# A graph layer's gather of x[src]: more columns copied by ScalarE and VectorE, with 16-bit addresses

## The chip, the cores and the metric

The kernel runs on one core of one Trainium2 chip. A core has TensorE (matmuls, with their weight loads), VectorE (DVE in the profile), ScalarE (ACT), GpSimd (POOL) and SyncE (SP), each with its own instruction stream, and 16 DMA engines that move data when one of these streams issues a transfer. The time is device microseconds of one execution; the figure given is the median of several runs.

## The reference

There are 12,500 nodes with 64 features and 400,000 edges, sorted by their target `dst`. An edge's message is a two-layer network of the features of its source, of its target and of 16 edge attributes; messages are summed per target, and each node is updated and normalised.

```python
m_in = jnp.concatenate([x[src], x[dst], edge_attr], axis=-1)
h = jax.nn.silu(m_in @ W1 + b1)
messages = jax.nn.silu(h @ W2 + b2)
agg = jax.ops.segment_sum(messages, dst, num_segments=x.shape[0])
node_in = jnp.concatenate([x, agg], axis=-1)
return jax.nn.silu(node_in @ W3 + b3)
...
x = _layernorm(x + _L0_gnn_ref(x, edge_index, edge_attr_16, ...), axis=-1)
```

All is float32.

## The kernel before, in words

**Tiles and octets.** The 3,125 tiles of 128 edges are worked in 391 octets of 8 tiles (1,024 edges); three octets are a chunk. Because the edges are sorted by target, an octet touches a window of at most 48 consecutive nodes. A loop over `o` (line 626) issues the work of all stages, each stage for another octet; its engines TensorE, ScalarE, VectorE and SyncE run exactly the order that is written there (`manual_schedule`), and each of these streams is in order. The pools' buffer counts (lines 251 to 261) decide how far one stage may run ahead of the next.

**The part of x[src].** Before the loop has got far, the product of all x with the first 64 rows of W1 is put into a table `pa` in DRAM (`table`, lines 178 to 192). From octet 12 on (`RAW`), a tile's 128 rows of that table come in one of three ways:

- POOL issues one indirect DMA for a tile (`gather`, line 396), three octets ahead (`AHEAD`), into a tile `ga` of five buffers. TensorE transposes them into the PSUM tile `p1` (line 476).
- For one pair of tiles (256 edges) of some octets, listed in `pairs`, the features are copied column by column out of `xs`, which holds x transposed (a feature per partition, a node per column of 4 bytes). Each copy moves one node's column, 64 partitions by 4 bytes, to its edge's place in the tile `cx`: on VectorE a `tensor_reduce` (line 301), on ScalarE a `copy` (line 303). The address of the column is in a register. Registers are filled by a load of up to 16 addresses at a time (line 294; `LOADS` says how many by the first load of a part and by its later ones), which the engine's sequencer carries out itself. TensorE then multiplies `cx` by W1 (line 479).
- For one pair of tiles of some other octets, listed in `rpairs`, SyncE copies single rows of `pa`, 16 in each octet (`rows`, line 347).

**Addresses.** `index` loads the 256 source numbers of a pair as int32 into a tile `cxi` of one partition (SyncE, three octets ahead). `address` (line 382, VectorE, two octets ahead) turns them in place into byte addresses: 4 times the number plus `XADDR`, where `xs` begins in a partition. `xs` is held twice, in partitions 0 to 63 and 64 to 127; the first 128 edges of a pair are copied from the lower copy and the last 128 from the upper, whose address carries the partition in its upper bits (`XBASE`). `resident` (line 146) loads both copies.

**How columns are dealt out.** `ACOLS` and `VCOLS` give the columns per octet: ScalarE 32 ahead of its silu `h` (line 483) and 28 ahead of its silu `m` (line 498); VectorE 32 between `oh` and `xw`, and 32 behind `eh`. The sum, `RATE`, is 124. A pair takes part in the octet that comes one octet after its last column could be written.

**The other stages of an octet.** SyncE loads the targets of a chunk into `dr` and its attributes into `oh` (`load`, lines 435 and 436, two octets before the chunk; two buffers each) and the window's x into `xr` (line 415, three octets ahead). VectorE adds the sums of an octet six back to `agg` (line 512), compares targets with window nodes (`oh`, line 447, one octet ahead; `eh`, line 453), and masks the window's product (`xw`, line 425). TensorE, by octet: the window's product (line 420), transposes or column products of the sources, window and attributes (line 480), the sums of the octet four back (line 507), the bias and second layer of the octet two back (lines 492 and 494). ScalarE: columns, `h`, columns, `m`.

**Nodes.** 25 groups of up to 512 nodes are finished as soon as their sums are complete, one about every 16 octets: load, product on TensorE (`node_product`, lines 541 and 542, into a PSUM tile of the pool `mis` with two buffers, which the window products use too), silu on ScalarE (`node_silu`, line 548), statistics, division and store. `todo` lists them by octet; they come at the end of that octet's work, silu directly behind the product.

Of the kernel before, what the change touches and what calls it, by code (L numbers as in the profile page):

```python
# [9 lines left out]
F32 = mybir.dt.float32  # L10
BF16 = mybir.dt.bfloat16
I32 = mybir.dt.int32
U8 = mybir.dt.uint8
AF = mybir.ActivationFunctionType
OP = mybir.AluOpType
AX = mybir.AxisListType
# [2 lines left out]
ENG = mybir.EngineType  # L19

P = 128
# [9 lines left out]
LAST = 6  # L31
RAW = 12
TABLES = 7
ACOLS = (32, 28)
VCOLS = (32, 32)
ROWS = 16
LOADS = (16, 8)
XBASE = (0, 64 << 18)
XADDR = 36864
LAG = CT * P // 32  # L40

U = 125
# [58 lines left out]
def windows(ctx, tc, ident, badi, pa, x, xt, src_c, src_row, dst_c, dst_row, attr_t, dst_2, attr_2, base, w1, b1, w2, b2, w3, b3, out, edges):  # L101
    nc = tc.nc
    N, D = x.shape
    NP = xt.shape[1]
    A = attr_t.shape[0]
    TILES = edges // P
    NO = base.shape[1]
    assert 2 * (S + A) == P and N + S <= NP
    E = 2 * S
    const = ctx.enter_context(tc.tile_pool(name="fconst", bufs=1))  # L110

    fast = ctx.enter_context(tc.tile_pool(name="fast", bufs=1))
    scp = ctx.enter_context(tc.tile_pool(name="scp", bufs=3))
    srcs = {}

    def sources(k, part=None):
# [22 lines left out]
    for s in range(2):  # L139
        h = slice(s * D, (s + 1) * D)  # L140
        nc.scalar.dma_start(w1d[h, h], w1[0:D, :])
        nc.scalar.dma_start(b1s[h, :], b1.rearrange("(k o) -> k o", o=1))
    XC = 2048
    xs = fast.tile([P, NP], F32, name="xs")

    def resident(s, c):
        w = min(XC, NP - c)
        nc.scalar.dma_start(xs[s * D:(s + 1) * D, c:c + w], xt[:, c:c + w])

    resident(0, 0)  # L150
    for s in range(2):
        h = slice(s * D, (s + 1) * D)
        nc.scalar.dma_start(w2d[h, h], w2)
    resident(0, XC)
    w3x = const.tile([D, D], F32, name="w3x")
    b3r = const.tile([1, G, D], F32, name="b3r")

# [88 lines left out]
    octs = []  # L246
# [4 lines left out]
    with tc.tile_pool(name="gat", bufs=AHEAD + 2) as gat, tc.tile_pool(name="drp", bufs=2) as drp, \  # L251
# [4 lines left out]
            tc.tile_pool(name="ps1", bufs=2, space=PSUM) as ps1, \  # L256
            tc.tile_pool(name="ps2", bufs=2, space=PSUM) as ps2, \
            tc.tile_pool(name="psa", bufs=1, space=PSUM) as psa, \
            tc.tile_pool(name="cx", bufs=4) as cx, tc.tile_pool(name="cxi", bufs=3) as cxi, \
            tc.tile_pool(name="rx", bufs=2) as rx, tc.tile_pool(name="rxi", bufs=2) as rxi, \  # L260
            tc.tile_pool(name="nx", bufs=2) as nx, tc.tile_pool(name="nv", bufs=1) as nv:
        got, loaded, made = {}, {}, {}
# [2 lines left out]
        RATE = sum(ACOLS) + sum(VCOLS)  # L265
        pairs = []
        while True:
            o = RAW + -(-2 * P * (len(pairs) + 1) // RATE) + 1
            if o >= len(octs) - 1:
                break  # L270
            pairs.append(o)
        cols, indices = {}, {}
        xb = xs.bitcast(U8)

        def columns(o, eng, part):
            if o < RAW:
                return
            lo = (o - RAW) * RATE
            if eng == ENG.Activation:
                lo, n = lo + sum(ACOLS[:part]), ACOLS[part]  # L280
            else:
                lo, n = lo + sum(ACOLS) + sum(VCOLS[:part]), VCOLS[part]
            hi, todo = lo + n, n
            while lo < hi:
                j, e0 = lo // (2 * P), lo % (2 * P)
                if j >= len(pairs):
                    return
                n = min(hi - lo, P - e0 % P, LOADS[lo > hi - todo])
                if pairs[j] not in cols:
                    cols[pairs[j]] = cx.tile([P, P], F32, name="cx")  # L290
                t = cols[pairs[j]].bitcast(U8)
                s = e0 // P
                h = slice(s * D, (s + 1) * D)
                _, regs = nc.values_load_multi_w_load_instructions(  # L294
                    indices[j][0:1, e0:e0 + n], engines=(eng,), min_val=XBASE[s] + XADDR,
                    max_val=XBASE[s] + XADDR + 4 * (N - 1), skip_runtime_bounds_check_because="src names a node")
                for e, r in zip(range(e0 % P, e0 % P + n), regs):
                    to, frm = t[h, 4 * e:4 * e + 4], xb[h, ds(r - (XBASE[s] + XADDR), 4)]
                    if eng == ENG.DVE:

                        nc.vector.tensor_reduce(to, frm[:, :, None], AX.X, OP.max)  # L301
                    else:
                        nc.scalar.copy(to, frm)  # L303
                lo += n


        def begun(o):

            first, behind = -(-(o - RAW) * RATE // (2 * P)), -(-(o + 1 - RAW) * RATE // (2 * P))
            return range(max(0, first), max(0, min(behind, len(pairs))))  # L310

        def index(o):
            for j in begun(o):
                t = cxi.tile([1, 2 * P], I32, name="cxi")
                e = octs[pairs[j]][1] * P
                nc.sync.dma_start(t, src_row[:, e:e + 2 * P])
                indices[j] = t

        def address(o):
            for j in begun(o):  # L320
                t = indices[j]
                for s in range(2):
                    h = slice(s * P, (s + 1) * P)
                    nc.vector.tensor_scalar(t[:, h], t[:, h], 4.0, float(XBASE[s] + XADDR), op0=OP.mult, op1=OP.add)

        rpairs = []
        while True:
# [48 lines left out]

        def address(o):
            for j in begun(o):
                t = indices[j]
                for s in range(2):  # L380
                    h = slice(s * P, (s + 1) * P)
                    nc.vector.tensor_scalar(t[:, h], t[:, h], 4.0, float(XBASE[s] + XADDR), op0=OP.mult, op1=OP.add)

        winrow, winreg = {}, {}
        sums = psa.tile([P, 4, S], F32, name="pg")
# [38 lines left out]
        def window_copy(o):  # L424
            nc.vector.tensor_tensor(xw[o % 3][:E, :], winrow.pop(o)[:E, :], mask[:E, :], op=OP.mult)  # L425

        def load(c, o0=0, o1=CT // OT):

            if c not in loaded:
                loaded[c] = (drp.tile([E, CT // 2 * P], I32, name="dr"), hot.tile([P, CT // 2 * P], F32, name="oh"))  # L430
            dr, oh = loaded[c]
            e = slice(o0 * OT // 2 * P, o1 * OT // 2 * P)
            d = slice(c * CT // 2 * P + e.start, c * CT // 2 * P + e.stop)
            for k in range(2):
                nc.sync.dma_start(dr[k * S:(k + 1) * S, e], dst_2[k:k + 1, d].to_broadcast([S, e.stop - e.start]))
            nc.sync.dma_start(oh[E:, e], attr_2[:, d])

# [12 lines left out]
        def compare_nodes(o):  # L450
            c, t0, n, first, last = octs[o]
            eh = ehp.tile([P, OT, S], F32, name="eh")
            nc.vector.tensor_tensor(eh[:, :n], row[:, None, :].to_broadcast([P, n, S]),  # L453
                                    rel[:, t0:t0 + n, None].to_broadcast([P, n, S]), op=OP.is_equal)
            hots[o].append(eh)
# [54 lines left out]
        def add_window(o):  # L510
            a = agg[:, ds(winreg.pop((ENG.DVE, o)), S)]
            nc.vector.tensor_tensor(a, a, sums[:, o % 4, :], op=OP.add)  # L512
# [32 lines left out]
        def node_silu(q):  # L545
            p = groups[q][1] // G
            z = nx.tile([P, G, D], F32, name="z")
            nc.scalar.activation(z[:p], nodes[q][1][:p], AF.Silu)
            nodes[q].append(z)
# [32 lines left out]
        due = [-(-(c + n + LAG) // STEP) for c, n in groups]  # L582
        NCH = octs[-1][0] + 1
        lead = {c: o for o, (c, t, n, first, last) in enumerate(octs) if first}
        todo = {}

        def later(o, f, *a):
            todo.setdefault(min(o, NO), []).append((f, a))
# [4 lines left out]
        for q in range(early):  # L593
            o = lead[due[q]] + LAST - 1 if q < rest else NO
            later(o - 1, node_load, q)
            later(o, node_product, q)
            later(o, node_silu, q)
            later(o + 2, node_stats, q)
        for q0, q1 in batches:
            o = lead[due[q1 - 1]] + LAST - 1  # L600
# [22 lines left out]
        with tc.manual_schedule(engines={ENG.PE, ENG.Activation, ENG.DVE, ENG.SP}):  # L623
            compare_dst(0)
            compare_nodes(0)
            for o in range(NO + THIRD):
# [5 lines left out]
                    nc.scalar.activation(agg[:, k:k + n], zero.to_broadcast([P, n]), AF.Copy)  # L632
                if o < 2:
                    for c in parts[2:5] if o == 0 else parts[5:]:
                        resident(0, c)
                if o == 3:
                    for s in range(2):
                        nc.scalar.dma_start(w3s[s * D:(s + 1) * D, :], w3[D:2 * D, :])
# [4 lines left out]
                if o == RAW:  # L643
                    nc.vector.memset(mv, 1.0)
                    nc.vector.memset(eps, 1e-5)
                if 5 <= o < 5 + (len(parts) + 1) // 2:
                    for c in parts[(o - 5) * 2:(o - 4) * 2]:
                        resident(1, c)
                index(o + 3)
                rload(o + 3)  # L650
                if o % (SCT // OT) == 6 and (o // (SCT // OT) + 1) * SCT < TILES:
                    sources(o // (SCT // OT) + 1)
                if o + AHEAD < NO:
                    gather(o + AHEAD)
                if o + 2 < NO and octs[o + 2][3] and o + 2:
                    load(octs[o + 2][0])
                if o + 3 < NO:
                    window_load(o + 3)
                if o + 1 < NO:
# [7 lines left out]
                columns(o, ENG.DVE, 0)  # L667
                if o < NO:
                    first_layer(o)
                if o == 0:  # L670
                    nc.vector.tensor_copy(b2r, b2p[:, None, :].to_broadcast([3, OT, D]))
                if o + 1 < NO:
                    window_copy(o + 1)
                    compare_nodes(o + 1)
                columns(o, ENG.DVE, 1)
                if o == 1:
                    relative(CT, SCT)
                if 10 <= o < 9 + len(cuts):
# [38 lines left out]

        for o in range(NO + THIRD - LAST, NO):
            add_window(o)
        for f, a in todo.get(NO, []):  # L720
            f(*a)
        for q in range(early, NG):
            node_load(q)
            node_product(q)
            node_silu(q)
            node_stats(q)
# [262 lines left out]
```

## Time and profile before

| | |
|---|---|
| median of 3 runs | 3,443.22 us (3,439.3 to 3,445.99) |
| profiled execution | 3,453.06 us, span of the profile 3,450.7 us |
| TensorE busy (weight loads) | 74% (48%), mean granted clock 0.68 |
| VectorE busy | 73% |
| ScalarE busy | 79% |
| POOL busy | 74% |
| 16 DMA engines | 67 GB/s on average |
| gathers of POOL | 2,619 from `pa`, 96 from x in the first 12 octets |
| columns | 24,032 on VectorE, 22,560 on ScalarE |

A group of the profile is read as: line, engine, operation, output and input, count, then busy time in us and mean ns of one, then the engine's idle time just before these instructions and what ended most of it. "issue" is idle time that ended without anything the profile shows as a wait. Register loads and the issue of DMAs do not count as busy; the view of a single line shows them, with their durations. Copies of columns overlap in their engine: one takes 188 ns from start to end on ScalarE, while the next starts about 93 ns after it.

### The profile page before, as it was taken

To read this page: it belongs to the slowest core of one execution; us is meant where nothing else is said; L and a number is where in the kernel's file an instruction comes from. 1 tells how busy PE (TensorE), PEld (TensorE's weight loads), DVE (VectorE), ACT (ScalarE), POOL (GpSimd) and SP (SyncE) were. 2 spreads that over 40 slices of the span, in tenths; PEclk is the share of its full clock that TensorE was granted. 3 is DMA by queue.
4 is the path that set the end of the run, shared out by engine and by line. 5 is a ranking of instruction groups with operands and counts; after the bars stand their busy time and mean duration, and the time that the engine had idled before them with its cause. 6 is when DMAs were issued, how large, how long until landed. Compare 5 with 4: busy or idle time off the path is not lost. (4 is left out here: it accounts for less than half of the span.)

```text
span 3450.7 us, 104586 instructions
## 1 busy us (share of the span) xinstructions
PE 2554.8 (74%) x13750; PEld 1649.2 (48%) x13750; DVE 2517.4 (73%) x26396; ACT 2717.7 (79%) x23405; POOL 2569.0 (74%) x2724
## 2 busy tenths in 40 slices
PE   6877777777777677776777777777777677677777
PEld 4444544444445445444444445444445454444454
DVE  2477777777777777777777777777777777777775
ACT  2388788788887887888878888887788777878886
POOL 7777777777777777777777777777777777777773
PEclk9666667666667666776666666666666666766767
DMA  7423323323332332333332332333323323333322
GB/s 159 95 53 68 63 59 65 65 61 60 77 61 61 68 62 60 65 65 65 64 69 59 62 68 61 62 75 61 62 60 69 60 61 66 69 62 62 67 61 52
DMA packets 203931, 229.79 MB, mean 67 GB/s; under 512 B 133612, under 2 KB 141988, under 8 KB 202324
## 3 DMA queue, kind: packets, MB, share of 16 engines
q1 hardware_dynamic: 101528, 122.61, 16.1%
q0 software_dynamic: 86880, 89.14, 14.1%
q10 hardware_dynamic: 14812, 11.26, 1.4%
q14 instruction: 595, 4.87, 0.5%
q8 instruction: 116, 1.90, 0.2%
HBM read 216.36 MB, written 6.40 MB: 65 GB/s over the span
## 5 line engine op out<-in xcount | busy, mean ns | idle before, releaser
L396 POOL DMA_INDIRECT ga<-pa,sc x2619 | 2475.4, 945 | 802.2 <-issue 711.9
L303 ACT COPY cx<-xs 64x4 uint8 x22560 | 2216.5, 188 | 166.8 <-issue 122.0
L301 DVE TENSOR_REDUCE cx<-xs 64x4 uint8 x24032 | 1782.6, 150 | 544.7 <-issue 477.8
L507 PEld LDWEIGHTS pg<-eh,m 128*64 128x64 f32 x6250 | 301.0, 182 | 1046.8 <-issue 331.1
L507 PE MATMUL pg<-eh,m 128*64 128x48 f32 x6250 | 351.3, 271 | 580.9 <-DVE agg L512 523.0
L480 PE MATMUL p<-oh,xw 128*128 128x512 f32 (+1 forms) x758 | 601.0, 887 | 132.3 <-DVE xw L425 130.0
L494 PE MATMUL p<-w2d,h 128*128 128x128 f32 x3126 | 674.8, 383 | 0.0
L494 PEld LDWEIGHTS p<-w2d,h 128*128 128x128 f32 x3126 | 573.8, 275 | 133.1 <-issue 133.1
L498 ACT ACTIVATE m<-p 128x512 f32<-128x512 f32 x391 | 232.2, 594 | 255.5 <-PE p L494 249.0
L447 DVE TENSOR_TENSOR oh<-dr,wrow 96x512 f32<-96x512 int32 x391 | 264.4, 676 | 209.1 <-DMA dr<-in_dst 121.6
L483 ACT ACTIVATE h<-p,b1s 128x512 f32<-128x512 f32 x391 | 267.3, 684 | 139.2 <-PE p L480 86.1
L476 PE MATMUL p<-ident,ga 128*128 128x128 f32 x1310 | 336.9, 389 | 41.4 <-DMA ga<-pa,sc 41.4
L420 PE MATMUL mm<-w1bb,xr 64*96 64x128 f32 x782 | 252.9, 418 | 62.0 <-DMA xr<-in_xt 36.7
L476 PEld LDWEIGHTS p<-ident,ga 128*128 128x128 f32 x1310 | 199.6, 190 | 133.3 <-issue 110.3
L480 PEld LDWEIGHTS p<-oh,xw 128*128 128x128 f32 x758 | 176.7, 287 | 169.3 <-DVE xw L425 168.8
L453 DVE TENSOR_TENSOR eh<-wrow,dc 128x384 f32<-128x384 f32 x391 | 211.7, 541 | 0.0
L420 PEld LDWEIGHTS mm<-w1bb,xr 64*96 64x96 f32 x782 | 134.2, 224 | 140.2 <-issue 61.4
L492 PE MATMUL p<-b2r,one 3*128 3x512 bf16 x391 | 196.4, 502 | 0.0
L512 DVE TENSOR_TENSOR agg<-agg,pg 128x48 f32 x391 | 78.1, 200 | 74.2 <-PE pg L507 40.0
L479 PE MATMUL p<-cx,w1d 128*128 128x128 f32 x364 | 105.2, 387 | 22.7 <-ACT cx L303 22.7
L425 DVE TENSOR_TENSOR xw<-mm,mask 96x128 f32<-96x128 f32 x391 | 109.4, 280 | 13.4 <-PE mm L420 7.6
L396 POOL DMA_INDIRECT ga<-in_x,sc x96 | 91.5, 953 | 30.2 <-issue 27.7
(83 smaller groups left out, 767.6 us busy)
## 6 DMA issues: line engine op xcount, KB each, us to landing
rx<-pa SPq DMA_DIRECT2D x5888, 0.2 KB
dr<-in_dst SPq DMA_DIRECT2D x260, 288.0 KB
ga<-pa,sc POOLq DMA_INDIRECT x2619
oh<-in_attr SPq DMA_DIRECT2D x130, 192.0 KB
xr<-in_xt SPq DMA_DIRECT2D x391, 24.0 KB
xs<-in_xt ACTq DMA_DIRECT2D x12, 512.0 KB
pa<-v ACTq DMA_DIRECT2D x12, 256.0 KB
xa<-in_x SPq DMA_DIRECT2D x24, 128.0 KB
```

What stands on the lines that cost most here:

```text
L301: nc.vector.tensor_reduce(to, frm[:, :, None], AX.X, OP.max)
L303: nc.scalar.copy(to, frm)
L396: nc.gpsimd.indirect_dma_start(out=ga[:, i, :], out_offset=None, in_=x if o < RAW else pa[:, :], in_offset=bass.IndirectOffsetOnAxis(ap=sc ...
L420: nc.tensor.matmul(pw[:E, :], winrow[o].rearrange("k s w -> k (s w)"), w1bb.rearrange("k s m -> k (s m)"), start=True, stop=True)
L447: nc.vector.tensor_tensor(oh[:E, :], dr[:, e:e + w], wn[:E, o:o + 1].to_broadcast([E, w]), op=OP.is_equal)
L453: nc.vector.tensor_tensor(eh[:, :n], row[:, None, :].to_broadcast([P, n, S]), rel[:, t0:t0 + n, None].to_broadcast([P, n, S]), op=OP.is_equal)
L476: nc.tensor.matmul(p1[:, i, :], g2.rearrange("p s d -> p (s d)"), ident, is_transpose=True, start=(i == c), stop=False, skip_group_check=True)
L480: nc.tensor.matmul(p1[:, :k], xw[o % 3], oh, start=False, stop=True, skip_group_check=True)
L483: nc.scalar.activation(h[:, :k], p1[:, :k], AF.Silu, bias=b1s)
L494: nc.tensor.matmul(p2[:, 2 * i:2 * i + 2, :].rearrange("p s d -> p (s d)"), h[:, i, :], w2d, start=False, stop=(i == k - 1), skip_group_ch ...
L498: nc.scalar.activation(m[:, :n2], p2[:, :n2], AF.Silu)
L507: nc.tensor.matmul(pg[s * D:(s + 1) * D, :], m[:, i, :], eh[:, i, :], start=(i < 2), stop=(i >= n - 2), skip_group_check=True)
```

## The change

- **Addresses are 16-bit numbers.** `address` writes them to a new tile `cxa` (uint16, three buffers) in one instruction for all 256. To fit into 16 bits, `xs` moves to the front of SBUF (`XADDR` 8864 instead of 36864; its own pool is opened first, and the area for the descriptors of POOL's DMAs is cut to 8,192 bytes of a partition), and it is held once, in partitions 0 to 63. Columns of the last 128 edges of a pair are read there and written to partitions 64 to 127.
- **Loads.** Every load of addresses takes up to 16.
- **Columns.** ScalarE 72 (40 and 32), VectorE 88: 24 ahead of `xw`, 16 between `xw` and `eh`, 24 and 24 behind. `RATE` is 160.
- **An octet moved.** A pair takes part two octets after its last column could be written; `dr` and `oh` are loaded three octets before their chunk; `node_silu` stands behind the `h` of the next octet.
- **Buffers.** `cx` five instead of four, `cxi` two instead of three, `sc` two instead of three.

In ScalarE's order, an octet has two loads of 16 and one of 8 for the first 40 columns and two of 16 for the other 32; in VectorE's, each 24 columns have a load of 16 and one of 8. In the whole kernel, VectorE has 32,912 columns with 2,618 loads (1,496 of them ahead of 16 columns, 1,122 ahead of 8) where it had 24,032 with 2,391; ScalarE 26,992 with 1,968 where it had 22,560 with 2,352. POOL has 2,515 gathers from `pa`.

```diff
-ACOLS = (32, 28)
-VCOLS = (32, 32)
+ACOLS = (40, 32)
+VCOLS = (24, 16, 24, 24)
 ROWS = 16
-LOADS = (16, 8)
-XBASE = (0, 64 << 18)
-XADDR = 36864
+LOADS = (16, 16)
+XADDR = 8864
...
+    front = ctx.enter_context(tc.tile_pool(name="front", bufs=1))
+    xs = front.tile([P, NP], F32, name="xs")
...
-    scp = ctx.enter_context(tc.tile_pool(name="scp", bufs=3))
+    scp = ctx.enter_context(tc.tile_pool(name="scp", bufs=2))
...
-    def resident(s, c):
+    def resident(c):
         w = min(XC, NP - c)
-        nc.scalar.dma_start(xs[s * D:(s + 1) * D, c:c + w], xt[:, c:c + w])
+        nc.scalar.dma_start(xs[:D, c:c + w], xt[:, c:c + w])
...
-            tc.tile_pool(name="cx", bufs=4) as cx, tc.tile_pool(name="cxi", bufs=3) as cxi, \
+            tc.tile_pool(name="cx", bufs=5) as cx, tc.tile_pool(name="cxi", bufs=2) as cxi, tc.tile_pool(name="cxa", bufs=3) as cxa, \
...
-            o = RAW + -(-2 * P * (len(pairs) + 1) // RATE) + 1
+            o = RAW + -(-2 * P * (len(pairs) + 1) // RATE) + 2
...
                 _, regs = nc.values_load_multi_w_load_instructions(
-                    indices[j][0:1, e0:e0 + n], engines=(eng,), min_val=XBASE[s] + XADDR,
-                    max_val=XBASE[s] + XADDR + 4 * (N - 1), skip_runtime_bounds_check_because="src names a node")
+                    addresses[j][0:1, e0:e0 + n], engines=(eng,), min_val=XADDR,
+                    max_val=XADDR + 4 * (N - 1), skip_runtime_bounds_check_because="src names a node")
                 for e, r in zip(range(e0 % P, e0 % P + n), regs):
-                    to, frm = t[h, 4 * e:4 * e + 4], xb[h, ds(r - (XBASE[s] + XADDR), 4)]
+                    to, frm = t[h, 4 * e:4 * e + 4], xb[:D, ds(r - XADDR, 4)]
...
         def address(o):
             for j in begun(o):
-                t = indices[j]
-                for s in range(2):
-                    h = slice(s * P, (s + 1) * P)
-                    nc.vector.tensor_scalar(t[:, h], t[:, h], 4.0, float(XBASE[s] + XADDR), op0=OP.mult, op1=OP.add)
+                addresses[j] = cxa.tile([1, 2 * P], U16, name="cxa")
+                nc.vector.tensor_scalar(addresses[j], indices.pop(j), 4.0, float(XADDR), op0=OP.mult, op1=OP.add)
...
-            later(o, node_silu, q)
+            behind.setdefault(o + 1, []).append(q)
             later(o + 2, node_stats, q)
...
-                if 5 <= o < 5 + (len(parts) + 1) // 2:
-                    for c in parts[(o - 5) * 2:(o - 4) * 2]:
-                        resident(1, c)
...
-                if o + 2 < NO and octs[o + 2][3] and o + 2:
-                    load(octs[o + 2][0])
+                if o + 3 < NO and octs[o + 3][3]:
+                    load(octs[o + 3][0])
...
                 columns(o, ENG.DVE, 0)
                 if o < NO:
                     first_layer(o)
+                for q in behind.get(o, []) if o < NO else []:
+                    node_silu(q)
...
                 if o + 1 < NO:
                     window_copy(o + 1)
+                    columns(o, ENG.DVE, 1)
                     compare_nodes(o + 1)
-                columns(o, ENG.DVE, 1)
+                    columns(o, ENG.DVE, 2)
+                columns(o, ENG.DVE, 3)
...
+        for q in behind.get(NO, []):
+            node_silu(q)
         for f, a in todo.get(NO, []):
             f(*a)
+            if f is node_product:
+                node_silu(*a)
...
-    nc = bacc.Bacc("TRN2", target_bir_lowering=False, num_devices=1)
+    nc = bacc.Bacc("TRN2", target_bir_lowering=False, num_devices=1, dynamic_dma_scratch_size=8192)
```

## The prediction

> **What bounds the kernel now.** I read the page's busy shares first (they decide nothing: 73 to 79% on four engines), then the groups, the waits by engine, a table of nine 200 us stretches, and last the timeline of some octets.
>
> From the page, busy times and groups:
>
> ```profile
> PE 2554.8 (74%) x13750; PEld 1649.2 (48%) x13750; DVE 2517.4 (73%) x26396; ACT 2717.7 (79%) x23405; POOL 2569.0 (74%) x2724
> ...
> L396 POOL DMA_INDIRECT ga<-pa,sc x2619 | 2475.4, 945 | 802.2 <-issue 711.9
> L303 ACT COPY cx<-xs 64x4 uint8 x22560 | 2216.5, 188 | 166.8 <-issue 122.0
> L301 DVE TENSOR_REDUCE cx<-xs 64x4 uint8 x24032 | 1782.6, 150 | 544.7 <-issue 477.8
> ```
>
> The stretches (busy us and instruction counts of each engine), and the timelines of POOL and VectorE:
>
> ```profile
> 1000.00:1200.00 200.00, 143.41 (x776) 90.52 (x776) 148.97 (x1597) 162.15 (x1421) 151.19 (x161) 0.68 0.29 61
> 1800.00:2000.00 200.00, 146.13 (x791) 94.05 (x789) 149.19 (x1598) 166.68 (x1457) 151.21 (x161) 0.69 0.32 64
> ```
>
> ```profile
> 1603.21 0.94 POOL L396 DMA_INDIRECT ga<-pa,sc  x1 [0.30 <-issue]
> 1604.45 0.94 POOL L396 DMA_INDIRECT ga<-pa,sc  x1 [0.30 <-issue]
> ```
>
> ```profile
> 1614.11 1.00 DVE L572 TENSOR_SCALAR v<-v,mv,rstd 128x64 f32<-128x64 f32 x4
> 1615.03 0.19 DVE L512 TENSOR_TENSOR agg<-agg,pg 128x48 f32 x1
> 1615.15 0.67 DVE L447 TENSOR_TENSOR oh<-dr,wrow 96x512 f32<-96x512 int32 x1
> 1615.74 1.72 DVE L301 TENSOR_REDUCE cx<-xs 64x4 uint8 x24
> 1617.80 0.59 DVE L301 TENSOR_REDUCE cx<-xs 64x4 uint8 x8 [0.34 <-issue]
> 1618.32 0.27 DVE L425 TENSOR_TENSOR xw<-mm,mask 96x128 f32<-96x128 f32 x1
> 1618.51 0.54 DVE L453 TENSOR_TENSOR eh<-wrow,dc 128x384 f32<-128x384 f32 x1
> ```
>
> The reader should see that POOL issues 161 gathers in every 200 us, one each 1.242 us (0.94 busy, 0.30 between), whatever the rest does; waits of another kind are 62 us in the whole run. An octet has 8 tiles; 124 columns and 16 rows of it come another way, so POOL issues 8 - 140/128 = 6.906 gathers, which is 8.58 us an octet. 2,715 gathers are 3,372 of the 3,450.7 us. POOL bounds the kernel. The others follow by octet (23.3 octets in 200 us): ScalarE 163/23.3 = 7.0 us busy, VectorE 150/23.3 = 6.45 busy plus 477.8/379 = 1.26 "issue", TensorE 6.4. SyncE's 16 rows take 5.14, their address load 1.42, xr 0.65, with shares of dr, oh and cxi about 7.9.
>
> The "issue" idle is the address loads at L294, which the page does not count as busy. The view of that line, in narrow stretches of the trace (VectorE with 16 and with 8 addresses), the load of four window bases, and the lone load of one number at the end:
>
> ```profile
> L294 DVEq TENSOR_LOAD <-cxi x1: 1100/1100/1100, 1614.5 to 1614.5; - x1
> ...
> L294 DVEq TENSOR_LOAD <-cxi x1: 594/594/594, 1616.2 to 1616.2; - x1
> ...
> L404 DVEq TENSOR_LOAD <-bi x98: 340/344/761, 50.5 to 3424.8; - x98
> ...
> L95 DVEq TENSOR_LOAD <-badi x1: 309/309/309, 3442.9 to 3442.9; - x1
> ```
>
> **The change, part by part.**
>
> *More columns.* 160 instead of 124 per octet: 59,904 columns in place of 46,592, so 52 more pairs of tiles and 104 gathers fewer: 104 x 1.242 = 129 us off POOL, 8.23 us an octet. This is the ceiling of the gain.
>
> *ScalarE.* 12 more copies. In an uninterrupted row, 32 copies last 3.08 us, (3.08 - 0.19)/31 = 0.093 each: +1.12, 8.1 us busy. Of its idle time, the 122 us of "issue" shrink with shorter loads, and 123.2 us (24 waits of 5 us by z at L548 for the node product) go, because node silu now stands behind the next octet's h. What is late next there is m, which waits for TensorE today too (249 us). The product's PSUM buffer is held until then; the next TensorE instruction that takes it is the window product two octets on, so I cost the hold at nothing; without that cover it is the 26 us that L420 waits for z now. ScalarE comes to about 8.15.
>
> *VectorE.* 24 more reduces. Eight last 0.59 to 0.62 us with a 0.15 us tail, 0.064 each: +1.53 on 6.45 is 7.98. The addresses of a pair cost one instruction of 256 (333 ns by the like one at L363) instead of two of 128 (240 ns): 234 x 0.333 against 364 x 0.24, nothing. Decisive is what the loads now cost. Their number goes from 2,391 to 2,618 on VectorE (1,496 of 16 and 1,122 of 8) and from 2,352 to 1,968 on ScalarE. No row shows a 16-bit load. Its ends: 16 addresses cost between 594 ns (they are as many bytes as eight today) and 1,100; eight between 344 and 594. The rows for one, four, eight and sixteen numbers, 309, 344, 594, 1,100, are steps of about 250 per started four, and a single number costs nearly a full step. That looks like a read of 16 bytes at a time, with (344 - 309)/3 = 12 ns for each register. By bytes, 16 need two steps and eight more registers than the 594 row, some 690 at most. I take 650 and 370, nearer the low end.
>
> A load delays VectorE by what queued work does not cover. Today 1.26 us over 6.3 loads an octet. In the new order, 24 | xw | 16 | eh | 24 | 24 columns, loads behind oh (0.67) and eh (0.54, after 16 reduces) are covered; those behind xw (0.27) and behind eight reduces (0.51) stick out by 0.3 and 0.1. Four gaps fewer also take four tails of 148 - 64 = 84 ns out of the busy time. 7.98 + 0.4 - 0.34 = 8.05; with nothing exposed 7.6, with today's 0.2 per load 9.0.
>
> The sequencer alone: two loads of eight start 0.92 us apart, so eight reduces take it 0.04 us each. 1,496 x 0.65 + 1,122 x 0.37 = 1,387 us, 3.66 an octet, and 97 instructions 3.9: 7.55, less than 8.05.
>
> The Trainium skill, page "Runtime: NRT & Kernel Launch", section "Instruction fetch mechanics", prices such loads at about 200 ns per register, even in bulk. By that the width of a number would not matter; the rate itself is not that of the trace, 64 to 86 ns for four and more. The case is rival 3.
>
> *x once, at partitions 0 to 63.* Seven loads of x go, all in the first octets beside other work: 0, at most the 9.5 us that h once waited for a load of that queue. Half of the columns now read partitions 0 to 63 and write 64 to 127. No row shows that: at one end 0; at the other each such reduce waits for the one before, 148 instead of 64 ns, 44 x 0.084 = 3.7 us an octet. I take 0, as either half today runs at the 64 ns pitch.
>
> The Trainium skill, page "VectorE: DVE Perf Modes", section "Two Vector instructions with no wait between them", lets an instruction wait for its predecessors only if the quadrant of its input or of its output differs from the last one's. Inside a run of columns both stay the same, so by it the price is 0; no run here shows it yet.
>
> *dst an octet earlier.* The waits of oh for dr (121.6 us, 71 times) are largely gone where VectorE becomes late. With two buffers, the attr load must now wait until TensorE's L480 of the octet just before; behind it in SyncE's queue are xr and 16 rows. Held up to 3 us once in three octets, covered because xr is used two octets later and the rows a pair (16 octets) later; uncovered it is 1 us an octet. SyncE also issues 52 more cxi (0.25 each, 13 us, hidden), and loses its 44.7 us of waits for ScalarE to release cxi.
>
> *Pairs an octet later, five cx, two cxi, three cxa, two sc, a smaller descriptor area for POOL.* They move buffers, not work: 0. If POOL had to wait for descriptors, its 0.30 us gap would grow; 2,611 x 0.07 us would undo the gain. TensorE does 52 x 2 passes for 52 transposes more: 20 us beside its 26% idle.
>
> **Sum.** POOL 8.23, ScalarE 8.15, VectorE 8.05, SyncE 7.9: four in-order engines that lay 0.7 us and more below POOL come within 0.3 of each other. Octets are uneven (a node group adds about 5 us to TensorE once in 16), so I add 2%, an estimate: 8.40. (8.58 - 8.40) x 379 = 68 us. The profiled run took 3,453.06 us (2.4 around its span), so 3,385; the median of the runs is 10 lower: 3,375.
>
> **Rivals.**
> 1. POOL stays the only bound: 3,443 - 129 = 3,314. For: today it loses hardly anything to the others. Against: their margin falls from 8% to some 2%. 11%.
> 2. The engines hinder each other by 4% and more: 8.50 to 8.65, 3,413 to 3,470. For: the chain of waits already runs through dr, rows and TensorE, and L507 waits 523 us for agg on VectorE, which comes behind 48 more columns' worth of queue. 18%, and half of it is slower than before.
> 3. Slower: the load costs by the number of addresses. 1,496 x 1.1 + 1,122 x 0.597 = 2,315 us, 6.1 an octet, with 3.9 for the instructions 10.0 on VectorE's sequencer: +1.43 x 379 = 542, about 3,985. It decides from where loads exceed 8.58 - 3.9 = 4.7 us an octet, that is 16 addresses at some 830 ns. For: four addresses, not 16 bytes, explain the steps as well. Against: the near-equal price of one and four. 15%.
> 4. Reading and writing across partitions holds VectorE: 8.05 + 3.7 = 11.8, about 4,650. 4%.
>
> **How the numbers follow.** The forecast has 52%. The range 3,305 to 3,490 holds it and rivals 1 and 2; left out are 3 and 4, 19%. Within 0.2% (7 us, about what a measurement can tell here) only rival 2 falls: 5%. Faster: 52 + 11 + 5 = 68%. Slower: 8 + 15 + 4 = 27%.
>
> **What would show it.** Right: 2,611 gathers, still with mostly a 0.30 us gap but some waits for TensorE's release of ga; VectorE loads of 16 at 600 to 700 ns, of 8 at 340 to 400; "issue" before the reduces below 200 us; z without its 5 us waits; oh without dr waits. Wrong: loads of 16 at 1,100 ns; reduces in a pitch above 64 ns; POOL with a longer gap; SyncE waiting long for L480.

## The result

The changed kernel took 9,173.7 us (median of 4, 9,169.9 to 9,187.8) against 3,442.4 us before: 2.666 times as long, with a 95% interval of 2.661 to 2.670. The forecast was 3,375 us. The profiled execution has a span of 9,170.2 us.

### The profile after

Busy times and groups from the page of the changed kernel, with its own line numbers (L376 is the gather, L304 and L302 the columns on ScalarE and VectorE):

```profile
PE 3048.0 (33%) x13802; PEld 1921.4 (21%) x13802; DVE 3074.9 (34%) x35146; ACT 3288.5 (36%) x27837; POOL 2472.6 (27%) x2620
...
L302 DVE TENSOR_REDUCE cx<-xs 64x4 uint8 x32912 | 2335.2, 140 | 5928.5 <-issue 5919.3
L304 ACT COPY cx<-xs 64x4 uint8 x26992 | 2763.6, 188 | 3882.9 <-issue 3380.1
L376 POOL DMA_INDIRECT ga<-pa,sc x2515 | 2379.5, 946 | 6586.8 <-PE p L456 5669.3
```

No engine is busy for more than 36% of the span. VectorE now stands 5,919 us at "issue" ahead of its columns, where it stood 478. With its 3,075 us of work that is nearly the whole span. POOL, which had waited 11 us for TensorE to release `ga`, now waits 5,669: it no longer sets the pace, it follows.

The 200 us from 1,000 us on, in the same columns as the stretches before (POOL does 53 instructions there instead of 161), and the timelines of VectorE and POOL:

```profile
1000.00:1200.00 200.00, 69.10 (x293) 43.18 (x293) 66.81 (x772) 72.11 (x625) 50.13 (x53) 0.50 0.11 23
```

```profile
4004.68 1.11 DVE L302 TENSOR_REDUCE cx<-xs 64x4 uint8 x16 [3.00 <-issue]
4007.06 0.60 DVE L302 TENSOR_REDUCE cx<-xs 64x4 uint8 x8 [1.28 <-issue]
4007.69 0.29 DVE L405 TENSOR_TENSOR xw<-mm,mask 96x128 f32<-96x128 f32 x1
4011.03 1.10 DVE L302 TENSOR_REDUCE cx<-xs 64x4 uint8 x16 [3.05 <-issue]
...
4006.64 0.95 POOL L376 DMA_INDIRECT ga<-pa,sc  x1 [18.36 <-PE p L456]
```

Every run of columns in this stretch has 1.3 to 3.3 us of idle time in front of it, whatever stands before it. The 16 reduces themselves take 1.10 us, no longer than before. The view of the address loads (least, median and largest duration in ns) has the cause:

```profile
L295 DVEq TENSOR_LOAD <-cxa x2618: 1820/3583/3835, 130.5 to 9121.7; - x187
L295 ACTq TENSOR_LOAD <-cxa x1968: 1704/3368/3624, 131.9 to 9136.1; - x197
```

A load of 16 addresses that took 1,100 ns takes 3,583, and one of 8 takes 1,820 where it took 594. The loads alone are 1,496 x 3.583 + 1,122 x 1.82 = 7,402 us of VectorE's sequencer. The columns fill 59,904/160 = 374 octets (the prediction divides by all 379 from octet 12 on), so that is 19.8 us an octet. With the 3.9 us that the prediction counts for handing out the instructions it is 23.7 us. The measured octet is 24.0 us: the loads start from 130.5 to 9,121.7 us, 8,991 us for 374 octets. ScalarE's loads, four of 16 and one of 8, come to 4 x 3.37 + 1.70 = 15.2 us, so VectorE is the later of the two.

### The profile page after: what moved, and what is told of

It is laid out like the page before. It is cut to its first block, busy times and chain, and to the rows that moved or that the text cites. A ratio compares the mean times of both kernels' runs of the same rounds, so it can differ in the third digit from the quotient of the medians.

```text
span 9170.2 us, 117190 instructions
## 1 busy us (share of the span) xinstructions
PE 3048.0 (33%) x13802; PEld 1921.4 (21%) x13802; DVE 3074.9 (34%) x35146; ACT 3288.5 (36%) x27837; POOL 2472.6 (27%) x2620
## 5 line engine op out<-in xcount | busy, mean ns | idle before, releaser
L302 DVE TENSOR_REDUCE cx<-xs 64x4 uint8 x32912 | 2335.2, 140 | 5928.5 <-issue 5919.3
L304 ACT COPY cx<-xs 64x4 uint8 x26992 | 2763.6, 188 | 3882.9 <-issue 3380.1
L376 POOL DMA_INDIRECT ga<-pa,sc x2515 | 2379.5, 946 | 6586.8 <-PE p L456 5669.3
L487 PE MATMUL pg<-eh,m 128*64 128x48 f32 x6250 | 421.6, 306 | 5665.3 <-DVE agg L492 5634.9
L487 PEld LDWEIGHTS pg<-eh,m 128*64 128x64 f32 x6250 | 369.5, 218 | 6221.7 <-issue 3843.1
L460 PE MATMUL p<-oh,xw 128*128 128x512 f32 (+1 forms) x758 | 738.4, 1075 | 405.4 <-DVE xw L405 405.3
L474 PE MATMUL p<-w2d,h 128*128 128x128 f32 x3126 | 798.7, 436 | 0.0
L474 PEld LDWEIGHTS p<-w2d,h 128*128 128x128 f32 x3126 | 684.9, 323 | 167.9 <-issue 167.9
L460 PEld LDWEIGHTS p<-oh,xw 128*128 128x128 f32 x758 | 181.1, 297 | 519.8 <-DVE xw L405 519.8
L400 PE MATMUL mm<-w1bb,xr 64*96 64x128 f32 x782 | 282.7, 462 | 19.9 <-DMA xr<-in_xt 19.9
L400 PEld LDWEIGHTS mm<-w1bb,xr 64*96 64x96 f32 x782 | 150.2, 250 | 106.4 <-issue 99.7
L459 PE MATMUL p<-cx,w1d 128*128 128x128 f32 x468 | 145.0, 412 | 0.1
L459 PEld LDWEIGHTS p<-cx,w1d 128*128 128x128 f32 x468 | 126.3, 329 | 0.3 <-ACT cx L304 0.3
L405 DVE TENSOR_TENSOR xw<-mm,mask 96x128 f32<-96x128 f32 x391 | 109.5, 280 | 16.9 <-PE mm L400 11.1
L376 POOL DMA_INDIRECT ga<-in_x,sc x96 | 91.0, 948 | 30.3 <-issue 27.1
```

The lines of the kernel that those rows point to most:

```text
L376: nc.gpsimd.indirect_dma_start(out=ga[:, i, :], out_offset=None, in_=x if o < RAW else pa[:, :], in_offset=bass.IndirectOffsetOnAxis(ap=sc ...
L400: nc.tensor.matmul(pw[:E, :], winrow[o].rearrange("k s w -> k (s w)"), w1bb.rearrange("k s m -> k (s m)"), start=True, stop=True)
L459: nc.tensor.matmul(p1[:, 0, :], w1d, cols.pop(o), start=False, stop=False, skip_group_check=True)
L460: nc.tensor.matmul(p1[:, :k], xw[o % 3], oh, start=False, stop=True, skip_group_check=True)
L474: nc.tensor.matmul(p2[:, 2 * i:2 * i + 2, :].rearrange("p s d -> p (s d)"), h[:, i, :], w2d, start=False, stop=(i == k - 1), skip_group_ch ...
L487: nc.tensor.matmul(pg[s * D:(s + 1) * D, :], m[:, i, :], eh[:, i, :], start=(i < 2), stop=(i >= n - 2), skip_group_check=True)
```

## The experiments

**The width alone, and the columns alone.** The theory after the result (W): a load fetches 16-bit numbers singly. The rivals: the place of the new tile (P), or the number of added columns (C). First, the changed kernel with nothing but int32 in the address tile:

```diff
-                addresses[j] = cxa.tile([1, 2 * P], U16, name="cxa")
+                addresses[j] = cxa.tile([1, 2 * P], I32, name="cxa")
```

> The changed kernel with one edit: the address tile cxa holds int32 numbers again; place, buffers, 160 columns and all else stay. Theory W (the width does it: a 16-bit number is fetched alone, at 0.22 us each, an int32 four at a time): loads on VectorE go from 3,583 and 1,822 ns back to 1,100 and 594, its sequencer to 10.0 us an octet, time 3,850 to 4,050 us. Rival P (the place does it: a fresh tile of another pool, x in front of it, or the smaller descriptor area): loads stay at 3.6 us and the time near 9,170.

Measured: 4,086 us, 1.186 times the kernel before (1.184 to 1.189). Its loads:

```profile
L295 DVEq TENSOR_LOAD <-cxa x2618: 591/1095/1125, 139.7 to 4038.8; - x187
```

The count of loads is the same, the pool and its place too, and the loads are back at 591 and 1,095 ns. P falls. Of the 5,731 us that the change lost, 5,087 are the width of the numbers in one tile. The remaining 643 us go with the columns: 160 at int32 prices need 6.1 us of loads and 3.9 for the instructions, 10.0 us of VectorE's sequencer by sum, and the octet took (4,038.8 - 139.7)/374 = 10.4.

Second, the changed kernel with the columns and loads of before, 16-bit and int32:

```diff
-ACOLS = (40, 32)
-VCOLS = (24, 16, 24, 24)
+ACOLS = (32, 28)
+VCOLS = (32, 0, 32, 0)
-LOADS = (16, 16)
+LOADS = (16, 8)
```

> The changed kernel with the columns and loads of before (32 and 28 on ScalarE, 32 and 32 on VectorE, loads of 16 and then 8), addresses still 16-bit. W and P: VectorE's loads cost 681 x 3.58 + 1,525 x 1.82 + the shorter ones = 5,430 us, 14.3 us an octet, with 2.9 for its instructions 17.2: about 6,700 us. Rival C (the added columns overload the engines, the loads only follow): close to before, 3,450 to 3,600.

> As the run with 124 columns and 16-bit addresses, but with int32 addresses: what is left of the change is x once, dst, node silu and pairs an octet later, and the buffers. W: POOL bounds as before at 8.58 us an octet, 3,443 within 20 us. P: as slow as with 16 bits, about 6,700.

Measured: 6,848 us with 16 bits (1.989, 1.984 to 1.994), 3,438 us with int32 (0.9984, 0.9974 to 0.9994). VectorE's loads in the first and in the second of them:

```profile
L295 DVEq TENSOR_LOAD <-cxa x2377: 940/1824/3818, 128.8 to 6792.0; - x199
```

```profile
L295 DVEq TENSOR_LOAD <-cxa x2377: 339/597/1324, 135.1 to 3364.3; - x199
```

So C falls as well, as the cause of the large loss: without one added column 16 bits cost 3,410 us. The 6,700 us of the sum were 2% short. All the rest of the change, with columns as before, is worth about 0.2%: POOL still bounds. It did make room, though. TensorE's wait for gathered tiles, 41 us before, is now the longest wait of its matmuls:

```profile
PE p L456 <- DMA ga<-pa,sc: 628.3, 400, 6.1
```

**The loads by themselves.** 17 kinds of loads were added to VectorE's stream in the kernel before. In the first of two runs nothing used the loaded numbers, and the trace has none of these loads, only the waits in front of them. The time of that run, 3,448 us, says nothing.

> The kernel before, with 17 address loads, six times each, added behind its last octet on VectorE: int32 with 1, 2, 3, 4, 5, 8, 16 numbers, 4 from the second and 8 from the third number on, 16-bit with 1, 2, 4, 8, 16, 8 from the third on, 8-bit with 4 and 8. W: int32 in steps of 250 ns per started four, 16-bit at 62 + 220 ns for each, 8-bit the same as 16-bit. Rival B (steps of 16 bytes when the tile is well placed): 16-bit 8 near 344, 16 near 600. What no theory fixes: whether int32 that starts off a multiple of four costs more. Time about 30 us above before, without meaning.

In the second a small copy used each number (5,357 us, the added work included, beside 5,261 for the kernel before on the same chip, of which more below):

```diff
+        for _ in range(6):
+            use(nc.values_load_multi_w_load_instructions(pi[0:1, 0:1], **kw))
+            use(nc.values_load_multi_w_load_instructions(pi[0:1, 0:2], **kw))
...
+            use(nc.values_load_multi_w_load_instructions(pu[0:1, 0:16], **kw))
```

> As the run with added loads on VectorE in the kernel before, six times each, but every loaded number is now used by a small copy, so that the loads stay in the program: int32 with 1, 2, 3, 4, 5, 8, 16 numbers, 4 from the second and 8 from the third on, 16-bit with 1, 2, 4, 8, 16, 8 from the third on, 8-bit with 4 and 8. Theory W: int32 in steps of about 250 ns per started four numbers; 16-bit at 62 + 220 ns for each number whatever its place; 8-bit as 16-bit. Rival B (steps of 16 bytes, other tiles were badly placed): 16-bit with 8 near 344, with 16 near 600. Left open by both: an int32 load that starts off a multiple of four.

The view of each added line; `pi` is int32, `pu` 16-bit, `pb` 8-bit. In order: int32 with 1, 2, 3, 4, 5, 8 and 16 numbers; int32 with 4 from the second and with 8 from the third on; 16-bit with 1, 2, 4, 8, 16 and with 8 from the third on; 8-bit with 4 and 8. Durations are least, median and largest in ns:

```profile
L733 DVEq TENSOR_LOAD <-pi x6: 311/326/569, 2.1 to 5304.0; - x6
L734 DVEq TENSOR_LOAD <-pi x6: 535/538/542, 3.8 to 5304.5; - x6
L735 DVEq TENSOR_LOAD <-pi x6: 741/742/744, 4.6 to 5305.3; - x6
L736 DVEq TENSOR_LOAD <-pi x6: 345/352/689, 5.8 to 5306.5; - x6
L737 DVEq TENSOR_LOAD <-pi x6: 593/600/615, 13.8 to 5307.4; - x6
L738 DVEq TENSOR_LOAD <-pi x6: 592/598/610, 16.7 to 5309.0; - x6
L739 DVEq TENSOR_LOAD <-pi x6: 1095/1096/1101, 30.2 to 5310.6; - x6
L740 DVEq TENSOR_LOAD <-pi x6: 972/976/982, 52.3 to 5313.6; - x6
L741 DVEq TENSOR_LOAD <-pi x6: 1840/1854/2414, 53.8 to 5315.1; - x6
L742 DVEq TENSOR_LOAD <-pu x6: 297/300/700, 64.8 to 5317.9; - x6
L743 DVEq TENSOR_LOAD <-pu x6: 515/518/700, 67.6 to 5318.4; - x6
L744 DVEq TENSOR_LOAD <-pu x6: 942/946/956, 74.1 to 5319.2; - x6
L745 DVEq TENSOR_LOAD <-pu x6: 709/1825/1836, 78.8 to 5320.7; - x6
L746 DVEq TENSOR_LOAD <-pu x6: 3586/3594/4216, 87.5 to 5323.5; - x6
L747 DVEq TENSOR_LOAD <-pu x6: 1823/1826/1832, 93.0 to 5329.4; - x6
L748 DVEq TENSOR_LOAD <-pb x6: 693/960/977, 96.2 to 5332.2; - x6
L749 DVEq TENSOR_LOAD <-pb x6: 1830/1834/1840, 103.9 to 5333.7; - x6
```

This bears W out and corrects its int32 half; rival B falls. Two and three int32 numbers cost 538 and 742, more than four at 352: single numbers cost some 210 to 220 each, and four of a load that begins on a multiple of four cost 250 together, 1.2 times a single one. Eight int32 numbers begun at the third cost 1,854 instead of 598, which is about 80 + 8 x 220: every one goes singly, though the middle four of them are a group that a load begun elsewhere would join. The 16-bit and 8-bit numbers go singly wherever they begin, at about 80 + 220 ns for each. So the time follows neither bytes nor started groups of four. It fits a count of separate reads in which int32 numbers are joined by whole fours, and only where the load itself begins on a multiple of four.

**What the rest is worth with int32.** Three kernels with columns that suit the loads: the changed kernel with 136 and with 144 columns, and the kernel before with 136 and nothing moved.

```diff
-VCOLS = (24, 16, 24, 24)
+VCOLS = (16, 16, 16, 16)
...
-                addresses[j] = cxa.tile([1, 2 * P], U16, name="cxa")
+                addresses[j] = cxa.tile([1, 2 * P], I32, name="cxa")
```

(For 144 columns `VCOLS = (16, 16, 24, 16)`; in the kernel before `ACOLS = (40, 32)`, `VCOLS = (32, 32)`, `LOADS = (16, 16)`.)

> The changed kernel with int32 addresses and columns that suit their loads: ScalarE 40 and 32, VectorE four times 16, every load of 16; 2,585 gathers, 34 fewer than before. W, with POOL as the bound: 34 x 1.242 = 42 us less, about 3,400 (ScalarE at 8.15 and VectorE's sequencer at 4 x 1.1 + 2.9 = 7.3 us stay under POOL's 8.46). Rival 2 of the prediction (the engines hinder each other as soon as they come near POOL): 3,440 or more.

> The same with 8 more columns on VectorE (16, 16, 24, 16); 2,563 gathers. If POOL still bounds, 56 x 1.242 = 70 us less than before, 3,374. VectorE's sequencer takes 4 x 1.1 + 0.6 + 81 x 0.04 = 8.2 us an octet against POOL's 8.39; the run with 160 columns lay 0.3 above that sum, which makes 8.5 and about 3,415. Rival 2: 3,450 or more.

> The kernel before with the 136 columns alone (ScalarE 40 and 32, VectorE 32 and 32, every load of 16), x still twice, dst, node silu and pairs not moved: 2,585 gathers. If the moved parts are worth nothing, as I summed them, it equals the run with 136 columns and the moves. If dr and z come late once POOL is faster, it is 20 to 60 us slower than that run.

These three gave 5,348, 5,406 and 5,406 us beside 5,261 for the kernel before on the same chip, and they say nothing of the moves. ScalarE and VectorE stood far longer at "issue" ahead of their columns on that chip: 1,495 and 1,441 us with 136 columns and nothing moved, against 55 and 499 for the same kernel on another. Why stays open. Single instructions and loads took their usual time (a gather 944 ns against 945, loads of sixteen int32 1,097 in both), so the view of the loads above, from the same chip, counts. The same three kernels on another chip:

> The changed kernel with int32 addresses and columns that suit their loads (ScalarE 40 and 32, VectorE four times 16, all loads of 16), again, because in the first try the kernel before itself took 5,261 us: its sequencers stood still for 0.5 us and more between instructions there, in every engine. 2,585 gathers, 34 fewer than before. POOL as the bound: 42 us less, about 3,400. Rival 2: 3,440 or more.

> The same with 8 more columns on VectorE (16, 16, 24, 16), again for the same reason; 2,563 gathers. POOL as the bound: 70 us less, 3,374. VectorE's sequencer 8.2 us an octet by sum, 8.5 with the surplus of the 160-column run: 3,415. Rival 2: 3,450 or more.

> The kernel before with the 136 columns alone (40 and 32, 32 and 32, all loads of 16), again for the same reason; x twice, dst, node silu and pairs not moved. If the moves are worth nothing it equals the 136-column run with the moves; if dr and z come late once POOL is faster, 20 to 60 us slower than it.

| kernel | us | ratio to before, 95% interval |
|---|---|---|
| changed, int32, 136 columns | 3,419.8 | 0.992 (0.991 to 0.994) |
| changed, int32, 144 columns | 3,456.7 | 1.003 (1.002 to 1.004) |
| before, 136 columns, nothing moved | 3,493.8 | 1.013 (1.012 to 1.015) |

With the moves 136 columns take 0.8% less than the kernel before, without them 1.3% more: the two kernels with 136 columns are 74 us apart, where the moves did next to nothing at 124. With 144, POOL has 22 gathers fewer yet and the time is 37 us longer. The waits of that run say why: POOL waits longer for free buffers, and TensorE stands 853 us for VectorE's `agg`:

```profile
PE pg L487 <- DVE agg L492: 853.3, 319, 6.9
...
DVE cx L302 <- issue: 580.1, 1062, 1.2
...
POOL ga L376 <- PE p L456: 93.7, 32, 7.4
```

VectorE itself hardly waits for another engine. From 1,000 to 3,000 us it is busy 1,574 us, stands 357 at "issue" ahead of columns, and waits some 20 us for others. So with 144 columns its own stream bounds, int32 loads included: 8.7 us an octet (229 octets in 1,995 us), where the sum in the expectation had 8.2, and 8.5 with the surplus of the 160-column run.

**Which move.** The 136-column kernel, with `dr` and `oh` loaded two octets ahead again:

```diff
-                if o + 3 < NO and octs[o + 3][3]:
-                    load(octs[o + 3][0])
+                if o + 2 < NO and octs[o + 2][3] and o + 2:
+                    load(octs[o + 2][0])
```

> The int32 run with 136 columns and all moves (3,420 us, ratio 0.992), with dr and oh loaded two octets before their chunk again, as before; all else of it stays. The 136 columns without any move took 3,494, and VectorE waited 215 us for dr there. Theory D (dst is what the moves are worth): most of the 74 us come back, 3,470 to 3,495, with dr waits of some 200 us. Rival N (node silu and pairs): 3,420 to 3,435, and few dr waits.

Measured: 3,411.4 us, 0.991 (0.989 to 0.993), the fastest of all kernels here, though its interval overlaps that of the run with dst moved. Theory D falls. Rival N has the time nearly right (3,420 was its low end), though not the few waits for dr that it expected. The waits with dst moved, and then with dst put back:

```profile
PEld mm L400 <- DMA xr<-in_xt: 562.7, 149, 9.3
PE mm L400 <- DMA xr<-in_xt: 447.8, 132, 10.3
...
DVE oh L427 <- DMA dr<-in_dst: 51.5, 22, 3.8
```

```profile
DVE oh L427 <- DMA dr<-in_dst: 193.6, 81, 4.5
...
PE mm L400 <- DMA xr<-in_xt: 57.7, 31, 12.4
```

Loading dst earlier takes 142 us of waits from VectorE and gives TensorE 390 more for `xr`. Neither sets the end: POOL, which does, waits for TensorE about as little in both. The 74 us come from the other parts: node silu, pairs an octet later with five `cx`, x once, the other buffers, or the finer split of VectorE's columns, in which the two kernels differ too. Where they are lost can be read in POOL's waits for TensorE, without the moves and then with them:

```profile
POOL ga L396 <- PE p L476: 98.4, 41, 7.8
```

```profile
POOL ga L376 <- PE p L456: 17.6, 33, 3.4
```

In the unmoved kernel some 80 of the 98 us are waits that end about 2 us behind a node group's silu, z, which there waits for the node product (75.1 us in all, 9.8 with the moves); with the moves POOL has no such waits behind z. This points to node silu. But TensorE's waits for a pair's columns fall as well, from 111 us to 1, and the parts were not tried one by one, so which of them it is stays open.

## Why the prediction was wrong, by its own steps

- **POOL as the bound, 1.242 us a gather:** right for the kernel before. The int32 run with 124 columns keeps its time, and 34 gathers fewer gave 25 to 32 us of the 42 counted for them. (POOL's waits of another kind were 93 us before, not 62; nearly all are the usual gap of 0.30.)
- **The price of a 16-bit load, 650 and 370 ns, is the step that failed.** It measured 3,583 and 1,820, 5.5 and 4.9 times as much, and an octet of VectorE took 24.0 us instead of 8.05. With these prices the prediction's own sum for the sequencer comes within 2% of that. Both ends between which the price for sixteen was sought, 594 and 1,100, were those of int32 loads; that a narrower number could cost more than a wider one was left out. The row that decided for the low end, one number at 309 ns beside four at 344, was read as a single 16-byte step. By the later run it is a single read that costs nearly as much as a joined one; two and three numbers, which no row of the trace showed, cost more than four.
- **Rival 3**, the load priced by the number of addresses, named the right mechanism with the wrong rate: it took int32's 69 ns per number and came to 3,985. That is 2.5% below the 4,086 us of the int32 run, in which loads do cost so much. The Trainium skill, page "Runtime: NRT & Kernel Launch", section "Instruction fetch mechanics", gives some 200 ns for each register; it speaks of the runtime's own loads from HBM. The 220 ns that single numbers cost here, from SBUF and of whatever width, agree with it; for whole fours of int32, 62 ns a number, the measurement decides. I had set the page's rate aside because the trace showed 64 to 86 ns, but all those rows were loads of whole fours. By its rate the loads would have been 32,912 x 0.2 = 6,600 us on VectorE, and with 374 x 3.9 us for the instructions and 180 us beside the columns the time an estimated 8,240.
- **VectorE's reduces at 0.064 us, ScalarE's copies at 0.093, and no price for reading partitions 0 to 63 and writing 64 to 127:** right. 16 reduces take 1.10 us with their tail, whichever half they write; 16 copies take 1.62, 0.095 each.
- **z's waits:** right. In the changed kernel they are 10.0 us in 2 waits instead of 123.2 in 24, and 9.8 us with int32 and 136 columns.
- **dst an octet earlier at nothing:** right in the sum, 3,420 with it against 3,411 without, wrong in the cover. `xr` was said to have two octets to spare behind the held SyncE; TensorE waited 448 us for it.
- **Moved parts at nothing:** true at 124 columns, where POOL bounds with room to spare. At 136, where the engines come close to each other, the kernel without them and with the coarser split takes 74 us more.
- **Rival 2**, engines that hinder each other near POOL's rate: POOL's waits with 136 unmoved columns (3,494 us) are of this kind. The 3,457 us of 144 columns lie in its range, but there VectorE's own stream was the limit. (Its lower end, 8.50 us, is 3.3% above POOL's 8.23, not 4%.)

Whether 160 columns would have taken 3,375 us, had a 16-bit load cost 650 ns, no run shows. The int32 run with 144 columns makes it doubtful: VectorE came out half a microsecond an octet above its sum there.

## What to carry to other kernels

The price of a register load here followed how many numbers it had to read singly, not its bytes: measure the operand type itself, with a few instructions in any kernel, before a design rests on it. When the trace has only sizes that are multiples of something, several rules fit the steps between them, and the bounds must then also hold the case that the new form gets none of the saving. By these runs, registers are best loaded from 32-bit numbers, in whole fours, from a multiple of four on.

## What the runs showed that I had not expected

- Two int32 numbers (538 ns) and three (742) load slower than four (352), and eight that start at the third number take 1,854 ns instead of 598.
- ScalarE's sequencer pays the same way: 3,368 ns for sixteen 16-bit numbers where sixteen int32 took 1,020. Only VectorE was tried with the other sizes.
- TensorE's mean granted clock fell from 0.68 to 0.52 as its busy share fell from 74% to 33%; the matmul of L460 (L480 before) took 1,075 ns instead of 887. VectorE, which bounds, hardly waits for TensorE (16.1 us for the sums of L487, 11.1 for L400), so the slower clock cost next to nothing that these runs show. The Trainium skill, page "TensorE: Matmul & The Clock Gate", section "Part 1: The HAM clock gate (the "warmup" mystery)", has the clock go to half after an idle window of about 3.4 us; 372 waits of 15.1 us on average ahead of L487, about one in every octet, agree with that.
